# Layer 0's input transposed by VectorE from a second, rearranged load instead of by TensorE

## The chip, the cores and the metric

The kernel runs on one core of a Trainium2 chip. The metric is the device time of one execution in microseconds. The kernel before has a median of 2174.7 us over three runs (2173.53 to 2179.28); the profiled execution spans 2173.4 us.

## The reference, cut to what matters

Four graph layers follow one another over x of shape (128 graphs, 64 nodes, 256 features), each as `x = layernorm(x + layer(x))`. Only layer 0, an attention over the nodes of a graph, is touched:

```
Wh = einsum('bnf,fo->bno', x, W)                 # W is 256 x 256
e  = leaky_relu(Wh@a1 [:, :, None] + Wh@a2 [:, None, :], 0.2)
e  = where(adj == 0, -inf, e)
h  = einsum('bij,bjo->bio', softmax(e, -1), Wh)
x  = layernorm(x + h)
```

Layer 1 is a four-headed attention over 512 edges with a softmax over segments, layer 2 a normalised adjacency followed by two linear maps with batch statistics, layer 3 a graph convolution followed by short LSTMs. The projection `x @ W` needs x with features on the partitions, while x arrives in memory with one token per row.

## The kernel before, in words

**Tiling.** The 8192 tokens are cut in 16 blocks `q` of 512 tokens. A block is a tile `xin` of 128 partitions x 4 x 256: partition p of piece c holds token 128 c + p (two graphs per piece). `A` is one large tile, 128 x 16 x 1024, that holds the activations of all blocks in SBUF; block q's slice `A[:, q, :]` is first written when layer 0 of that block ends. Until then its upper end serves as room for set-up tiles (`su.tile`), taken from the top of A downwards.

**Layer 0** is cut in steps, each a function of a block:

- `load_x(q)` (lines 126 to 128) loads the block into one of two buffers `xin`;
- `l0_a` (208 to 210) calls `transposed` (191 to 199): for each half k of the features four TensorE transposes of 128 x 128 against an identity into one PSUM bank `m` (L197), and one ScalarE copy of the bank into `tT` (L198). Per block that is 8 transposes, 8 weight loads and 2 copies;
- `l0_b` (212 to 223) multiplies `tT` with the weights (L218) and copies out (L220, L223); `l0_c` makes scores and exponentials; `l0_d` transposes the exponentials; `l0_e` (252 to 266) multiplies by Wh (L258), adds the result to `xin` (L261, VectorE), normalises (L92 to L97) into `A[:, q, :]`, and calls `load_x(q + 2)`, since the buffer of `xin` is now free.

**Buffers.** `tT` has a single buffer, which `l0_a` shares with `l1_t`, the same helper in layer 1. So `l0_a`'s `tT` can be written only when the last reader of the previous one, `l1_qv` of the block before (L283 and L286), has finished. The PSUM pool `m` has three banks, used in turn by all of these steps.

**The loop** (lines 647 to 664) runs layers 0, 1 and the first part of 2 interleaved. Each turn q handles eight halves b of layer 1's edge scores (`l1_graph`, L320 with the ScalarE relu L322), and between them the steps in `between`. At b = 0 come `l0_e(q + 1)` and `l0_a(q + 2)`, at b = 2 `l0_b(q + 2)`. In every second turn the list holds layer 1's softmax too (`l1_softmax`, `l1_sums`, `l1_weights`: the VectorE scans L337 to L346 and the reciprocal L360).

**Order.** `step` ties every step's instructions on TensorE behind the step before it, by `tc.issue_after(queue[-1])`, so TensorE's order is the order of the list. On the other engines and on the queue that issues DMAs (SyncE) the framework's planner decides: it takes instructions in the written order as they become ready in its own forecast of time, so a later one whose inputs are there can go ahead of an earlier one that waits. Each engine then runs its list strictly in order.

Of the kernel before, what the change touches and what calls it, by code (L numbers as in the profile page):

```python
# [8 lines left out]
F32 = mybir.dt.float32  # L9
# [8 lines left out]
P = 128  # L18
# [3 lines left out]
KD = D // P  # L22
# [6 lines left out]
QT = 512  # L29
# [12 lines left out]
def kernel(ctx: ExitStack, tc: tile.TileContext, i, out):  # L42
    nc = tc.nc
# [8 lines left out]
    A = main.tile([P, NQ, 2 * QT], F32, name="A")  # L52
# [59 lines left out]
    with ExitStack() as two:  # L112
# [5 lines left out]
        work = ph.enter_context(tc.tile_pool(name="work", bufs=2))  # L118
        ps = ph.enter_context(tc.tile_pool(name="ps", bufs=1, space=PSUM))

        def bank(shape, name="m", bufs=3):
            return (psm if name == "m" else ps).tile([P] + shape, F32, name=name, bufs=bufs)
# [3 lines left out]
        def load_x(q):  # L126
            xin[q] = xp.tile([P, PQ, D], F32, name="xin")
            nc.sync.dma_start(xin[q], x_view[q])

        class su:  # L130

# [15 lines left out]


        load_x(0)
        w0 = wa.tile([P, KD, D + 2], F32, name="w0")  # L150
        nc.scalar.dma_start(w0[:, :, :D], i["L0_gnn_W"].rearrange("(k p) c -> p k c", p=P))
# [7 lines left out]
        for s in range(2):  # L159
            nc.sync.dma_start(bd[s * N:(s + 1) * N, s * N:(s + 1) * N], i["adj"])  # L160
        load_x(1)

        wq = wa.tile([P, KD, D + HEADS], F32, name="wq")
# [23 lines left out]
        def own(q, shape, name):  # L187

            return work.tile(shape, F32, name=name, bufs=1) if q else su.tile(shape, F32, name)

        def transposed(src, q=1):

            t = own(q, [P, KD, QT], "tT")
            for k in range(KD):
                p_ = bank([PQ, P])
                for c in range(PQ):
                    nc.tensor.transpose(p_[:, c, :], src[:, c, k * P:(k + 1) * P], ident)  # L197
                nc.scalar.activation(t[:, k, :], p_.rearrange("p c t -> p (c t)"), AF.Copy)  # L198
            return t
# [6 lines left out]
        L0 = {}  # L206

        def l0_a(q):
            L0[q] = {"x": xin.pop(q)}
            L0[q]["xT"] = transposed(L0[q]["x"], q)  # L210

        def l0_b(q):
            xT = L0[q]["xT"]
# [38 lines left out]
        def l0_e(q):  # L252
            x, wh, eT, ri = (L0[q][n] for n in ("x", "wh", "eT", "ri"))
            for c2 in range(2):
                p_ = bank([2, D])
                for c in range(2):
                    g = 2 * c2 + c
                    nc.tensor.matmul(p_[:, c, :], eT[:, g, :], wh[:, g, :D], start=True, stop=True)  # L258
                for c in range(2):
                    g = 2 * c2 + c  # L260
                    nc.vector.scalar_tensor_tensor(x[:, g, :], p_[:, c, :], ri[:, g:g + 1], x[:, g, :],  # L261
                                                   op0=OP.mult, op1=OP.add)
            layernorm(token_major(q), x, PQ, nc.gpsimd)
            L0.pop(q)
            if q + 2 < NQ:
                load_x(q + 2)
# [243 lines left out]
        def setup_signs():  # L510
# [4 lines left out]
            for h in range(HEADS):  # L515
                r, c0 = slice((h % 2) * 64, (h % 2 + 1) * 64), CG - HEADS + h
                nc.vector.tensor_copy(apad[r, h // 2, c0:c0 + 1], acol[r, h // 2:h // 2 + 1])

        l0_a(0)
        setup_l0()  # L520
        nc.vector.tensor_scalar(mask, bd, 0.0, NEG, op0=OP.is_equal, op1=OP.mult)
        l0_b(0)
        setup_order()
        l0_c(0)
        l0_a(1)
        setup_ends()
        l0_b(1)
# [119 lines left out]
        for q in range(NQ):  # L647
            S = q // BPS - 1 if q % BPS == 0 else -1
            between = [
                [(l0_e, q + 1), (l0_a, q + 2)],  # L650
                [(sums, q if q else -1), (l1_softmax, S)],
                [(l1_sums, S), (l0_b, q + 2)],
                [(v_b, q - LAG - 1)],
                [(l1_weights, S), (l1_t, q + 1), (l0_c, q + 2)],
                [(sums, q), (l1_qv, q + 1, 0)],
                [(v_c, q - LAG - 1), (v_a, q - LAG)],
                [(l0_d, q + 2), (l1_qv, q + 1, 1)],
            ]
            for b in range(GQ):
                step(l1_graph, q, b)  # L660
                for do, n, *more in between[b]:
                    step(do, n, *more)
                if setup:
                    setup.pop(0)()
# [58 lines left out]
        q = 0  # L723
# [90 lines left out]
    work = ctx.enter_context(tc.tile_pool(name="work3", bufs=2, reuse_waits="tile"))  # L814
# [290 lines left out]
```

## Time and profile before

| what | value |
|---|---|
| median of three runs | 2174.7 us |
| TensorE busy | 2083.1 us (96%) |
| ScalarE busy | 946.2 us (44%) |
| VectorE busy | 863.1 us (40%) |
| GpSimd busy | 414.7 us (19%) |
| DMA | 169275 packets, 105.54 MB |
| L197 transposes from `xin` | 128, median 273 ns each |
| L198 copies to `tT` | 62, mean 597 ns (both layers) |

Busy time is the union of an engine's instructions, so overlapping matmuls count once. Busy shares are averages over the whole span; layer 0 lies in the first quarter of it, so its stages must be read by themselves. In listings of one engine in order of time the columns are start, duration of the merged group, engine, line, operation, output and inputs, shape and count; a bracket gives idle time ahead of the group and what ended it.

### The profile page before, as it was taken

How to read it: one execution, taken by the hardware profiler on the slowest of the kernel's cores; microseconds unless marked ns; L12 is line 12 of the kernel's file. 1: busy time of each engine (PE TensorE's matmuls, PEld its weight loads, DVE VectorE, ACT ScalarE, POOL GpSimd, SP SyncE). 2: the span in 40 equal slices, each digit the busy share in tenths (PEclk: the TensorE clock that was granted, in tenths of full speed). 3: DMA queues.
4: the chain of work that ended last, by engine and by line, in shares of the span. 5: the costliest groups of instructions: out<-in, count | busy, mean ns of one | idle time of the engine just before them, and what ended most of it. 6: DMA issues, size and time to landing. Idle time of an engine off the chain costs nothing.

```text
span 2173.4 us, 29437 instructions
## 1 busy us (share of the span) xinstructions
PE 2083.1 (96%) x11463; PEld 1340.8 (62%) x11463; DVE 863.1 (40%) x2054; ACT 946.2 (44%) x1825; POOL 414.7 (19%) x569
## 2 busy tenths in 40 slices
PE   6999999998999979999999999999999999999997
PEld 4667677775454444576576577477468468468466
DVE  7355555454543444134233323323323423423223
ACT  3766666765338153234233334333333333333332
POOL 1123332433210012011111111111211211202012
PEclk9999999999999979999999999999999999999999
DMA  4023213232222022012112101201201201201001
GB/s 124 20 42 52 50 44 50 52 52 42 42 86 59 0 87 79 0 44 67 46 31 66 60 29 54 73 14 55 88 10 58 89 4 60 73 1 59 20 5 54
DMA packets 169275, 105.54 MB, mean 49 GB/s; under 512 B 86832, under 2 KB 152368, under 8 KB 168880
## 3 DMA queue, kind: packets, MB, share of 16 engines
q1 hardware_dynamic: 167280, 101.70, 17.7%
q8 instruction: 90, 1.47, 0.3%
q0 software_dynamic: 1024, 1.05, 0.2%
q10 hardware_dynamic: 832, 0.92, 0.1%
q14 instruction: 49, 0.40, 0.1%
HBM read 59.59 MB, written 44.04 MB: 48 GB/s over the span
## 4 chain that ended last, share of the span: by engine, by line
PE 80%; ACT 6%; DVE 6%; DMA 3%; issue 2%; POOL 1%; SPq 1%; DVEq 0%; POOLq 0%; ACTq 0%
PE l L970 31%; PE l L976 19%; PE pz L707 5%; PE pz L772 4%; PE e L311 3%; PE g L909 2%; PE g L921 2%; PE m L283 2%; PE m L218 2%; PE m L286 2%; PE g L866 1%; DMA way<-st 1%; PE z L320 1%; PE m L401 1%; PE m L197 1%
## 5 line engine op out<-in xcount | busy, mean ns | idle before, releaser
L970 PE MATMUL l<-H,wih 128*128 128x256 f32 (+2 forms) x2496 | 789.2, 471 | 9.4 <-ACT gate_g L990 3.9
L970 PEld LDWEIGHTS l<-H,wih 128*128 128x128 f32 x2496 | 469.9, 190 | 302.3 <-issue 189.2
L976 PE MATMUL l<-hid,whh 128*128 128x256 f32 (+2 forms) x1536 | 436.2, 437 | 2.1 <-DVE hid L999 2.1
L976 PEld LDWEIGHTS l<-hid,whh 128*128 128x128 f32 x1536 | 291.8, 190 | 130.9 <-issue 61.2
L982 ACT ACTIVATE gate_i<-l,bias 128x256 f32<-128x256 f32 (+2 forms) x176 | 100.1, 569 | 517.8 <-PE l L976 445.9
L985 DVE TENSOR_TENSOR gate_i<-gate_i,gate_g 128x256 f32<-128x256 f32 (+2 forms) x96 | 48.5, 506 | 432.7 <-ACT gate_g L982 432.6
L986 POOL TENSOR_TENSOR cell<-gate_f,cell 128x256 f32<-128x256 f32 (+2 forms) x96 | 84.4, 880 | 670.6 <-ACT gate_f L982 663.4
L83 POOL TENSOR_TENSOR ln_rs<-ln_rs,mhalf 128x2 f32<-128x2 f32 (+2 forms) x97 | 79.1, 815 | 689.5 <-DVE ln_rs L95 689.1
L322 ACT ACTIVATE u<-z 128x1024 f32<-128x1024 f32 x128 | 130.4, 1026 | 57.4 <-PE z L320 56.6
L982 ACT ACTIVATE gate_g<-l,bias 128x256 f32<-128x256 f32 (+2 forms) x176 | 100.3, 570 | 98.3 <-PE l L970 50.1
L990 ACT ACTIVATE gate_g<-cell 128x256 f32<-128x256 f32 (+2 forms) x176 | 90.0, 511 | 88.7 <-DVE cell L989 45.7
L982 ACT ACTIVATE gate_o<-l,bias 128x256 f32<-128x256 f32 (+2 forms) x176 | 99.4, 565 | 61.9 <-PE l L976 54.0
L707 PE MATMUL pz<-A,w 128*128 128x512 f32 x256 | 113.1, 595 | 0.0
L989 DVE TENSOR_TENSOR cell<-gate_i,gate_g 128x512 f32<-128x512 f32 (+2 forms) x80 | 50.0, 624 | 138.1 <-ACT gate_g L982 137.9
L294 DVE TENSOR_TENSOR qs<-m,qs 64x256 fp32r<-64x256 f32 x128 | 54.0, 422 | 124.4 <-ACT qs L293 122.7
L320 PE MATMUL z<-gath_r,qs 128*128 128x512 f32 x256 | 99.4, 476 | 0.6 <-ACT u L322 0.4
L707 PEld LDWEIGHTS pz<-A,w 128*128 128x128 f32 x256 | 47.9, 190 | 55.3 <-issue 53.6
L283 PE MATMUL m<-wq,tT 128*128 128x260 f32 x256 | 72.4, 406 | 8.1 <-ACT yT L391 5.4
L982 ACT ACTIVATE gate_f<-l,bias 128x256 f32<-128x256 f32 (+2 forms) x96 | 51.1, 532 | 59.8 <-PE l L976 59.8
L999 DVE TENSOR_TENSOR hid<-gate_o,gate_g 128x256 f32<-128x256 f32 (+2 forms) x96 | 48.6, 507 | 67.8 <-ACT gate_g L990 39.8
L999 DVE TENSOR_TENSOR H<-gate_o,gate_g 128x512 f32<-128x512 f32 (+1 forms) x64 | 40.9, 639 | 80.7 <-PE l L970 68.5
L286 PE MATMUL m<-wv,tT 128*128 128x256 f32 x256 | 67.3, 386 | 0.6 <-ACT v L296 0.5
(241 smaller groups left out, 2515.2 us busy)
## 6 DMA issues: line engine op xcount, KB each, us to landing
way<-st SPq DMA_DIRECT2D x59, 256.0 KB
st<-way SPq DMA_DIRECT2D x236, 64.0 KB
xin<-in_x SPq DMA_DIRECT2D x16, 512.0 KB
ld<-table SPq DMA_DIRECT2D x16, 512.0 KB
x_dram<-y SPq DMA_DIRECT2D x16, 512.0 KB
x2r<-x_dram SPq DMA_DIRECT2D x32, 256.0 KB
x_dram<-A SPq DMA_DIRECT2D x64, 128.0 KB
x3r<-x_dram SPq DMA_DIRECT2D x64, 128.0 KB
```

The costliest lines, as they stand in the source:

```text
L283: nc.tensor.matmul(pq, xT[:, k, c * P:(c + 1) * P], wq[:, k, :], start=k == 0, stop=k == KD - 1)
L286: nc.tensor.matmul(pv[:, c % 2, :], xT[:, k, c * P:(c + 1) * P], wv[:, k, :], start=k == 0, stop=k == KD - 1)
L320: nc.tensor.matmul(z[:, k, :], L1[q]["qs"][c][:, s, k * P:(k + 1) * P], gath_r, start=True, stop=True)
L322: nc.scalar.activation(u, z, AF.Relu)
L707: nc.tensor.matmul(p_, w1[:, k, m * P:(m + 1) * P], A[:, q, k * QT:(k + 1) * QT], start=k == 0, stop=k == KD - 1)
L772: nc.tensor.matmul(p_, w2[:, k, m * P:(m + 1) * P], hidden(q, k), start=k == 0, stop=k == M1 - 1)
L970: nc.tensor.matmul(gates[n], wih[p][:, k, mw * P:(mw + 1) * P], Hw[:, k, :, s, :], start=k == 0, stop=not s and k == KD - 1)
L976: nc.tensor.matmul(gates[n], whh[p][:, k, m * P:(m + 1) * P], hid[:, k], start=False, stop=k == KD - 1)
L982: nc.scalar.activation(act[n], gates[n], AF.Tanh if n == "g" else AF.Sigmoid, bias=bias[:, p - 1, m:m + 1])
L986: nc.gpsimd.tensor_tensor(cell[:, j], act["f"], cell[:, j], OP.mult)
L990: nc.scalar.activation(act["g"], cell[:, j], AF.Tanh)
L999: nc.vector.tensor_mul(Hw[:, jj, :, s, :] if over else new[:, jj], o, t)
```

## The change

`load_x(q)`, for every block but the first, loads the input a second time, into the still unused slice `A[:, q, :]`. Eight DMAs, one for each quarter n of the partitions and half k of the features, put into partition 32 n + t the pieces of 32 features (128 bytes) that start at feature 128 k + 32 n, of the tokens 32 j + t for j from 0 to 15. So each square of 32 partitions x 32 columns of A holds 32 tokens by 32 features, and already stands in the quarter of the partitions where its features belong. One VectorE transpose in squares of 32 then gives `tT` as before. TensorE's transposes and ScalarE's copies of `l0_a` go, for 15 of 16 blocks. The first load into `xin` remains, for the residual addition in `l0_e`. Its purpose is to take work off TensorE and ScalarE.

```diff
         def load_x(q):
             xin[q] = xp.tile([P, PQ, D], F32, name="xin")
             nc.sync.dma_start(xin[q], x_view[q])
+            if q:
+
+                rows = i["x"][q * QT:(q + 1) * QT, :].rearrange("(j t) (k i f) -> i k t j f", t=32, k=KD, f=32)
+                for n in range(4):
+                    for k in range(KD):
+                        to = A[n * 32:(n + 1) * 32, q, k * QT:(k + 1) * QT]
+                        nc.sync.dma_start(to.rearrange("t (j f) -> t j f", f=32), rows[n, k])
...
         def l0_a(q):
             L0[q] = {"x": xin.pop(q)}
-            L0[q]["xT"] = transposed(L0[q]["x"], q)
+            if q:
+
+                L0[q]["xT"] = work.tile([P, KD, QT], F32, name="tT", bufs=1)
+                nc.vector.transpose(L0[q]["xT"].rearrange("p k t -> p (k t)"), A[:, q, :])
+            else:
+                L0[q]["xT"] = transposed(L0[q]["x"], q)
```

## The prediction

> **What bounds the kernel now.** I first read the page's busy shares and its chain of work that ended last, then the first 600 us in stretches of 30 us, because layer 0 lives only there.
>
> ```profile
> PE 2083.1 (96%) x11463; PEld 1340.8 (62%) x11463; DVE 863.1 (40%) x2054; ACT 946.2 (44%) x1825; POOL 414.7 (19%) x569
> ...
> PE 80%; ACT 6%; DVE 6%; DMA 3%; issue 2%; POOL 1%; SPq 1%; DVEq 0%; POOLq 0%; ACTq 0%
> ```
>
> ```profile
> core 0: us, PE busy (x) PEld busy (x) DVE busy (x) ACT busy (x) POOL busy (x), PEclk, DMA share, GB/s
> 190.00:220.00 30.00, 29.22 (x275) 21.76 (x274) 13.05 (x41) 21.38 (x49) 12.32 (x16) 1.00 0.48 75
> 220.00:250.00 30.00, 27.66 (x258) 21.02 (x256) 18.31 (x40) 20.20 (x47) 6.95 (x8) 1.00 0.11 36
> ```
>
> TensorE (PE) is the bound in the loop too: 29.2 and 27.7 of 30 us. The second stretch is a turn with layer 1's softmax, where VectorE (DVE) is fuller. So TensorE time taken out comes off the end, if VectorE delivers in time. One turn without the softmax shows the room, first on TensorE, then on VectorE:
>
> ```profile
> 265.49 1.03 PE L286 MATMUL m<-wv,tT 128*128 128x256 f32 x4
> 266.17 0.81 PE L320 MATMUL z<-gath_r,qs 128*128 128x512 f32 x2
> 266.82 1.89 PE L258 MATMUL m<-wh,eT 128*128 128x256 f32 x8
> 268.89 1.09 PE L197 MATMUL m<-ident,xin 128*128 128x128 f32 x8 [0.18 <-ACT spad L295]
> 269.74 0.72 PE L320 MATMUL z<-gath_r,qs 128*128 128x512 f32 x2
> 270.39 1.92 PE L311 MATMUL e<-u,apad 128*32 128x512 f32 x16
> 272.24 0.73 PE L320 MATMUL z<-gath_r,qs 128*128 128x512 f32 x2
> 272.81 3.65 PE L218 MATMUL m<-w,tT 128*128 128x258 f32 x16
> ```
>
> ```profile
> 265.77 0.88 DVE L294 TENSOR_TENSOR qs<-m,qs 64x256 fp32r<-64x256 f32 x2 [0.62 <-ACT qs L293]
> 267.63 0.43 DVE L294 TENSOR_TENSOR qs<-m,qs 64x256 fp32r<-64x256 f32 x1 [0.98 <-ACT qs L293]
> 268.09 1.66 DVE L261 SCALAR_TENSOR_TENSOR xin<-m,ri,xin 128x256 f32<-128x256 f32 x4
> ...
> 271.52 0.16 DVE L95 TENSOR_SCALAR ln_rs<-ln_mv 128x4 f32<-128x4 f32 x1
> ```
>
> The last reader of `tT` (L286) ends at 266.52; L218, which needs the new `tT`, starts at 272.81. VectorE is idle from 266.65 to 267.63, then busy until 271.68.
>
> For the added work I read the same operation elsewhere, and the issues of the DMA queue:
>
> ```profile
> L848 DVE STREAM_TRANSPOSE st<-hd x31: 700/705/712, 948.3 to 2138.7; 128x512 f32<-128x512 f32 x31
> ```
>
> ```profile
> 8.94 0.47 SPq L77 DMA_DIRECT2D w<-in_W1T  x1
> ...
> 9.96 0.51 SPq L64 DMA_DIRECT2D b<-in_L_gnn_b  x1
> ...
> 38.14 0.37 SPq L128 DMA_DIRECT2D xin<-in_x  x1
> ```
>
> Vectors of layer 2 (L64), written after the whole loop, are loaded at 9.96 us, ahead of block 2's `xin`, which waits for its buffer. So the planner lets a load go as soon as its destination is free.
>
> **What the skill says.** (1) VectorE: DVE Perf Modes, The three transpose paths: VectorE's transpose works in blocks of 32 x 32 alone and writes SBUF. That is why the DMA must deal the features to the quarters. The trace has its time: 705 ns for 512 columns. (2) TensorE: Matmul & The Clock Gate, Part 4: PE-mode transpose: some 275 ns in a kernel, the result lands in PSUM and wants a copy, and transposes don't count as activity for the clock. The trace agrees on the first (273 ns median latency; eight overlap in 1.09 us) and leans to the last: in the softmax turn, after a stretch of almost only transposes from 246.05, L311 takes 3.09 us at 251.56 where 1.85 is usual. (3) DMA: Bandwidth & Descriptors, Specifications: full rate needs 512 bytes or more per descriptor. The trace agrees: the pairs of `ld` loads (L372: 8192 pieces of 128 bytes) run from about 141.0 to 148.3 at 122 to 188 GB/s, while `xin` reaches 244 to 364.
>
> **The change part by part.**
>
> *Removed from TensorE, in the loop (14 blocks, 2 to 15).* Eight transposes. L258 starts at 266.82 and ends at 268.71; in this sequence the next group starts 0.15 before the modelled end of the last, so L320 would start at 268.56 instead of 269.74: 1.18 us per turn, of which 0.18 is the wait for a PSUM bank (ACT L295) that the transposes were first to meet. *Removed from ScalarE*: two copies, 2 x 0.597 = 1.2 us per turn. ScalarE is at 20 to 21 of 30 us and its L322 is mostly waiting for TensorE, so I count this at nothing.
>
> *Added to VectorE.* One transpose of 1024 columns. The slope from L294 (256 columns, 422 ns) to a same-kind operation of 512 (L332, 0.69 us) is 1.05 ns per column, so 705 + 512 x 1.05 = 1.24 us; at most 2 x 0.705 = 1.41. It waits for the columns and for L286 of the previous `tT`, 266.52. In the planner's order L294, L261 and the normalisation are written earlier, but at 266.65 none of them is ready: the last L294 waits for ScalarE's L293, which in turn stands behind the copy of v (L296) that begins when L286 ends. I expect the transpose in this gap: about 266.65 to 267.95. Behind it the last L294 moves by some 0.4 us, and so do L261 and the normalisation; the next reader of that L294, an L320 six halves on, and ScalarE's L295, which runs at 268.67 anyway, don't feel it. L218 could start at 271.63: 3.7 us of slack. In a softmax turn the same gap lies at 231.15 to 232.13; L95 then ends near 236.6, and L332, which waits for L330 (now ending 1.18 earlier, at 236.7), starts in time. So 1.18 in both kinds of turn.
>
> *Added DMAs.* Per block 8 x 512 = 4096 pieces of 128 bytes, 0.5 MB: half of an `ld` pair, so 7.3 / 2 = 3.7 us of all DMA engines, and 8 issues. At the median of the `st` loads (L853, 428 ns) that is 3.4 us of SyncE. For 15 blocks: 61440 pieces, 7.9 MB, 55 us of DMA and 51 of SyncE. Slices of A below the set-up room are free from the start, so by the L64 evidence most columns will be loaded in the first 100 us or so, tens of microseconds before use, and before the first `ld` at 139.5. Even if issued right after their `xin` (209.76 for the block used at 233.4), they land by about 209.8 + 0.4 + 3.4 + 3.7 = 217. Hidden, then.
>
> *Set-up (block 1) and the first turns.* From 10 to 50 us VectorE is the bound (9.89, 7.01, 9.96 and 8.46 of 10 us), and TensorE's eight transposes at 18.17 are hidden there: nothing is won and 1.24 us of VectorE added. Block 1's columns follow `xin` at 6.86, so they are issued to about 10.7 and land near 15; `acol`, read by VectorE at 15.25, is pushed from 7.28 to about 11. Bounds: 0 (VectorE's gaps between 20 and 30 us take it) and 3 us (a wait as well). I take 1. In the two first turns set-up still fills VectorE, so I count 0.5 each instead of 1.18.
>
> *Sum.* 12 x 1.18 + 2 x 0.5 - 1 = 14.2; 2174.7 - 14.2 = 2160.5 us.
>
> **Rivals.**
>
> *A: the transpose falls behind the normalisation.* If the planner's forecast has no gap, it starts at 271.68 and ends at 272.92, and L218 starts 0.1 to 0.3 later than before (semaphore included). In softmax turns it lies between L95 (236.18) and L332, which starts at 237.5 instead of 237.9: 0.2 to 0.4 won. With 7 turns of each and 1 us of set-up: 2174.7 + 2.1 - 1.4 + 1 = 2176. For it: L261 is written first. Against: the 0.98 us gap.
>
> *B: softmax turns give nothing.* Their VectorE is busy from 237.90 to 253.5 almost without a break, and TensorE waits there in small pieces (0.57 for L403, 0.45 for L93); a longer wait can bring the slow clock. Six full turns: 7.1 + 1 - 1 = 7.1 won, 2167.6.
>
> *C: the columns come late, slower.* SyncE is in order and waits up to 23.6 us for L403, up to 19.8 for the table. If the columns of every second block stand behind the `ld` loads (263.80 to 267.15), they follow that pair's transfer (7.3 us from about 265.3, so to 272.6) by 3.7, to 276.3; with 1.24 for the transpose L218 starts at 277.6, 4.8 later than before. 7 x 4.8 - 7 x 1.18 + 1 = 26: 2201. Against: a free destination.
>
> **How the numbers follow.** Forecast 0.62, A 0.15, B 0.13, C and other losses in set-up 0.10. The best case is 14 x 1.27 with some luck in the clock, about 2154; the upper end takes in B and A, with 2177. Under 2168.2 (0.3%): 0.62 and most of B, 0.72. Within: A and the rest of B, 0.17. Slower: 0.11.
>
> **What would show it.** L197 from `xin` x8 instead of x128; a VectorE STREAM_TRANSPOSE x15 of about 1.24 us at the new line, ahead of L261, waiting for TensorE's L286 and not for a DMA; L320 directly behind L258; no TensorE wait before L218; the two kinds of turns, 29.8 and 35.5 us between L197 groups (203.62, 233.39, 268.89), shorter by 1.2 each; the new issues mostly before 110 us. Wrong would be: a wait of L218 for VectorE (A), TensorE idle growing near L403 and L229 (B), a VectorE wait for a DMA into A (C), or a loop that starts more than 3 us later.

## The result, and the profile after

The changed kernel takes 2157.5 us, median of four runs (2154.84 to 2158.79), against 2176.23 us of the kernel before on the same chip. The ratio is 0.9912, with a 95% interval of 0.9894 to 0.9930: faster by 0.9%. 2160.5 was forecast.

The page of the changed kernel, busy shares and the chain of work that ended last (its line numbers are those of before + 7 from `load_x` on, + 12 behind `l0_a`):

```profile
PE 2066.8 (96%) x11343; PEld 1329.6 (62%) x11343; DVE 881.6 (41%) x2069; ACT 931.1 (43%) x1795; POOL 418.7 (19%) x569
...
PE 81%; DVE 7%; ACT 5%; DMA 3%; issue 2%; POOL 1%; SPq 0%; ACTq 0%; DVEq 0%; POOLq 0%
```

TensorE has 120 matmuls and 16.3 us less, ScalarE 30 instructions and 15.1 us less, VectorE 15 instructions and 18.5 us more (15 x 1.24 = 18.6). TensorE is still the bound at 96%, with a shorter span (2156.5 against 2173.4 us in the profiled executions). One turn without the softmax, on TensorE in order of time:

```profile
317.18 0.82 PE L332 MATMUL z<-gath_r,qs 128*128 128x512 f32 x2
317.83 1.89 PE L270 MATMUL m<-wh,eT 128*128 128x256 f32 x8
319.37 0.82 PE L332 MATMUL z<-gath_r,qs 128*128 128x512 f32 x2
320.12 1.92 PE L323 MATMUL e<-u,apad 128*32 128x512 f32 x16
321.97 0.73 PE L332 MATMUL z<-gath_r,qs 128*128 128x512 f32 x2
322.54 3.65 PE L230 MATMUL m<-w,tT 128*128 128x258 f32 x16
```

L332 stands directly behind L270, 1.54 us after its start; before, its counterpart L320 came 2.92 us after L258's start. L230 has no bracket: no wait took the place of the transposes. From L270's start to L230's it is 4.71 us, before 5.99. VectorE in the same turn:

```profile
316.77 0.88 DVE L306 TENSOR_TENSOR qs<-m,qs 64x256 fp32r<-64x256 f32 x2 [0.62 <-ACT qs L305]
317.68 1.25 DVE L220 STREAM_TRANSPOSE tT<-A 128x1024 f32<-128x1024 f32 x1
318.96 0.43 DVE L306 TENSOR_TENSOR qs<-m,qs 64x256 fp32r<-64x256 f32 x1
319.42 1.66 DVE L273 SCALAR_TENSOR_TENSOR xin<-m,ri,xin 128x256 f32<-128x256 f32 x4
...
322.85 0.16 DVE L95 TENSOR_SCALAR ln_rs<-ln_mv 128x4 f32<-128x4 f32 x1
```

The transpose fills the gap ahead of the last L306, and ends 3.6 us before L230 wants `tT`. L306 and L273 come 0.32 us later after L270's start than before (1.13 against 0.81, 1.59 against 1.27), and no wait of TensorE follows from that. The groups of the transposes and, in the queue's own view, of the second loads, with counts and durations in ns (least, median, most), first and last start:

```profile
L220 DVE STREAM_TRANSPOSE tT<-A x15: 1240/1245/1245, 22.8 to 440.2; 128x1024 f32<-128x1024 f32 x15
```

```profile
L135 SPq DMA_DIRECT2D A<-in_x x120: 312/487/1842, 7.2 to 279.3; - x120
```

To compare kernels I measure turns from one start of `l0_e`'s matmuls (L258, now L270) to the next. The first column is the end of set-up, at block 0's `l0_e`; the second is block 1's, with which the loop begins. Of the turns the table has the regular ones, five of each kind, and it shows why a turn is a better ruler than a median: turns without the softmax agree within 0.03 us between executions.

| kernel | set-up to the first L258 | the loop's first L258 | turns without softmax | turns with softmax | layer 2's first matmul | ratio to before, 95% |
|---|---|---|---|---|---|---|
| before | 28.60 | 53.96 | 29.77 | 33.9 x3, 35.5 x2 | 541.82 | |
| after | 31.11 | 56.59 | 28.49 | 32.75 x5 | 523.62 | 0.9894 to 0.9930 |
| after, again | 33.08 | 56.95 | 28.49 | 32.75 x5 | 520.38 | 0.9912 to 0.9942 |
| e1 | 29.61 | 53.48 | 28.50 | 32.75 x5 | 517.00 | 0.9878 to 0.9911 |
| e2 | 28.64 | 54.05 | 29.78 | 33.9 x3, 35.5 x2 | 542.07 | 1.0010 to 1.0023 |
| e3 | 30.82 | 56.38 | 28.50 | 32.75 x4, 34.2 | 521.27 | 0.9884 to 0.9916 |
| e4 | 32.76 | 56.64 | 29.77 | 33.9 x4, 35.5 | 540.41 | 0.9989 to 1.0002 |
| e5 | 33.77 | 59.33 | 30.0 to 30.15 | 33.07 to 33.54 | 540.93 | 1.0023 to 1.0040 |
| e6 | 37.01 | 62.58 | 28.50 | 40.8 to 43.0 | 591.05 | 1.0201 to 1.0250 |
| e7 | 33.72 | 59.02 | 29.91 to 30.07 | 33.3 | 549.22 | 1.0028 to 1.0059 |
| f1 | 31.31 | 56.43 | 28.50 | 33.3 x3, 33.5, 35.0 | 533.08 | 0.9978 to 0.9992 |
| f2 | 32.50 | 58.07 | 28.50 | 32.77 x4, 32.9 | 526.03 | 0.9911 to 0.9949 |
| f3 | 28.98 | 54.51 | 28.49 | 32.75 x5 | 522.06 | 0.9889 to 0.9918 |
| f4 (e1 again) | 29.15 | 54.16 | 28.50 | 32.75 x5 | 520.69 | 0.9879 to 0.9916 |

Turns of 35.5 us, and the odd 34.2 and 35.0, hold a stretch at a slow TensorE clock (before, 317.2 to 319 us: 0.55 of full speed granted; usual: 1.00).

### The profile page after: what moved, and what is told of

The parts are those of the page before. It is cut to its first block, busy times and chain, and to the rows that moved or that the text cites. A ratio compares the mean times of both kernels' runs of the same rounds, so it can differ in the third digit from the quotient of the medians.

```text
span 2156.5 us, 29415 instructions
## 1 busy us (share of the span) xinstructions
PE 2066.8 (96%) x11343; PEld 1329.6 (62%) x11343; DVE 881.6 (41%) x2069; ACT 931.1 (43%) x1795; POOL 418.7 (19%) x569
## 4 chain that ended last, share of the span: by engine, by line
PE 81%; DVE 7%; ACT 5%; DMA 3%; issue 2%; POOL 1%; SPq 0%; ACTq 0%; DVEq 0%; POOLq 0%
PE l L982 32%; PE l L988 19%; PE pz L719 5%; PE pz L784 4%; PE e L323 3%; PE g L921 2%; PE g L933 2%; PE m L295 2%; PE z L332 2%; PE m L298 2%; PE m L230 2%; PE g L878 1%; PE m L413 1%; DMA way<-st 1%; ACT A L891 1%
## 5 line engine op out<-in xcount | busy, mean ns | idle before, releaser
L334 ACT ACTIVATE u<-z 128x1024 f32<-128x1024 f32 x128 | 130.3, 1025 | 64.3 <-PE z L332 63.3
L332 PE MATMUL z<-gath_r,qs 128*128 128x512 f32 x256 | 100.9, 482 | 0.6 <-ACT u L334 0.4
L306 DVE TENSOR_TENSOR qs<-m,qs 64x256 fp32r<-64x256 f32 x128 | 54.1, 422 | 109.0 <-ACT qs L305 106.9
L721 DVE BATCH_NORM_STATS2 st<-pz 128x6 f32<-128x512 f32 x64 | 44.4, 697 | 59.5 <-PE pz L719 59.4
```

The costliest lines, as they stand in the source:

```text
L332: nc.tensor.matmul(z[:, k, :], L1[q]["qs"][c][:, s, k * P:(k + 1) * P], gath_r, start=True, stop=True)
L334: nc.scalar.activation(u, z, AF.Relu)
```

## The experiments

Theory: the gain is the time of eight transposes on a full TensorE, and it is whole because the VectorE transpose lands in a gap and the loads are hidden. Rivals: the gain is ScalarE's relief; the loads, or block 1, take back a part of it; the place on VectorE is of no weight.

**The changed kernel again**, beside the next three on one chip.

> The changed kernel once more, as the measure for the three beside it. Every theory: about 2157 us, 17 to 19 below the kernel before on the same chip.

Measured: 2156.38 us (before there: 2173.99). The result repeats.

**Dead TensorE transposes (e4).** The part of the gain that is TensorE's.

```diff
                 nc.vector.transpose(L0[q]["xT"].rearrange("p k t -> p (k t)"), A[:, q, :])
+                for k in range(KD):
+                    p_ = bank([PQ, P])
+                    for c in range(PQ):
+                        nc.tensor.transpose(p_[:, c, :], L0[q]["x"][:, c, k * P:(k + 1) * P], ident)
```

> The changed kernel, and in addition TensorE makes the eight transposes of each block as before, into PSUM banks that nothing reads; ScalarE's copies stay away. Theory 1 (the gain is TensorE's time): 14 x 1.1 to 1.2 us come back, so 2172 to 2176. Rival (the gain is ScalarE's relief, or a shorter chain to tT): stays at 2157 to 2162.

Measured: 2173.03 us against 2173.85, ratio 0.9995. TensorE in order of time:

```profile
360.05 1.89 PE L274 MATMUL m<-wh,eT 128*128 128x256 f32 x8
362.12 1.10 PE L224 MATMUL m<-ident,xin 128*128 128x128 f32 x8 [0.18 <-ACT spad L311]
362.98 0.70 PE L336 MATMUL z<-gath_r,qs 128*128 128x512 f32 x2
```

The group of 1.1 us and even its wait of 0.18 for a PSUM bank are back, and the regular turns are those of before to 0.03 us, slow stretches apart. The whole gain in them is TensorE's time. That the medians agree too is in part luck: e4's loop starts 2.7 us later than before's (56.64 against 53.96), and its first three turns are 3.0 us shorter together (85.2 against 88.2), because slow stretches that before has there are missing.

**Dead ScalarE copies (f2).** The complement.

```diff
                 nc.vector.transpose(L0[q]["xT"].rearrange("p k t -> p (k t)"), A[:, q, :])
+                for k in range(KD):
+                    nc.scalar.activation(A[:, q, k * QT:(k + 1) * QT], L0[q]["x"][:, 2 * k:2 * k + 2, :].rearrange("p c d -> p (c d)"), AF.Copy)
```

> The changed kernel, and in addition two ScalarE copies of 128 x 512 per block where the old ones stood, from xin into the already read slice of A, which nothing reads. Theory 1 (ScalarE's copies were hidden): 2156 to 2159, turns of 28.5 and 32.75 us. Rival (part of the gain is ScalarE's): 2160 to 2170, turns longer by up to 1.2.

Measured: 2161.35 us (2157.26 to 2162.0). By its time alone that is the rival's range, not the theory's. But the rival put the loss in the turns, and these are 28.50 and 32.77, those of the changed kernel: the copies cost these turns nothing. Its ratio to before (0.9911 to 0.9949) overlaps that of the changed kernel's repeat, and what its median has over 2157.5 lies outside the regular turns, spread too thin to be placed (the loop's first group at 58.07 against 56.59 and 56.95; from the last group of the loop to layer 2 55.3 us against 54.8 and 52.5; behind it 1634 against 1633).

**Loads without their use (e2).** `load_x` as in the change, `l0_a` as before.

```diff
         def l0_a(q):
             L0[q] = {"x": xin.pop(q)}
-            if q:
-                L0[q]["xT"] = work.tile([P, KD, QT], F32, name="tT", bufs=1)
-                nc.vector.transpose(L0[q]["xT"].rearrange("p k t -> p (k t)"), A[:, q, :])
-            else:
-                L0[q]["xT"] = transposed(L0[q]["x"], q)
+            L0[q]["xT"] = transposed(L0[q]["x"], q)
```

> The columns are loaded into A, but nothing reads them: xT comes from TensorE as before. Theory 1 (the loads are hidden): within 2 us of the kernel before, about 2176. Rival (61440 small pieces slow the other transfers or hold SyncE, and part of the gain pays for that): 4 to 10 us above the kernel before.

Measured: 2177.45 us against 2173.99, ratio 1.0016 (1.0010 to 1.0023), so 2 to 5 us more, between the two theories. But in the profile, which caught the slowest of the 20 executions (2181.27), layer 2 begins at 542.07, before at 541.82: the stage with the loads lost 0.25 us. The rest took 1637.4 instead of 1631.6, though no load of the change is left there and TensorE, ScalarE and GpSimd run the whole kernel in the order of before. So the loads are hidden where they run. Of the 5.8 us behind, 3.3 arise at one place near 1530 us. There VectorE's addition of `st`, a tile that is written to memory and read back, waits for its DMA, in before and in e2:

```profile
1529.69 0.69 DVE L884 TENSOR_TENSOR x2r<-st,x2r 128x512 f32<-128x512 f32 x1 [2.37 <-DMA st<-way]
```

```profile
1532.28 0.69 DVE L891 TENSOR_TENSOR x2r<-st,x2r 128x512 f32<-128x512 f32 x1 [4.00 <-DMA st<-way]
```

The `H` that TensorE needs stands behind it in VectorE's order, so TensorE waits 2.39 us instead of 0.76, and matmuls of 1.06 us instead of 0.70 follow. Another 1.0 arises in the same way near 1025 us. Over all profiles here these two waits of TensorE run from 0.5 to 2.4 us. With one profile of each kernel it stays open whether the loads have a part in that, and what the 2 to 5 us of the 20 executions are.

**No second load (e3).** VectorE transposes `xin` itself.

```diff
-            if q:
-                rows = i["x"][q * QT:(q + 1) * QT, :].rearrange("(j t) (k i f) -> i k t j f", t=32, k=KD, f=32)
...
-                nc.vector.transpose(L0[q]["xT"].rearrange("p k t -> p (k t)"), A[:, q, :])
+                nc.vector.transpose(L0[q]["xT"].rearrange("p k t -> p (k t)"), L0[q]["x"].rearrange("p c d -> p (c d)"))
```

> No second load; VectorE transposes xin itself in squares of 32, so the features are not dealt to their quarters and layer 0's projection reads another arrangement (this part of the computation is changed). TensorE, ScalarE and VectorE do the work of the changed kernel. Theory 1 (loads hidden): within 2 us of the changed kernel, about 2157, a little less if the loads hold up set-up. Rival (the loads cost): 4 to 10 us below the changed kernel.

Measured: 2151.46 us, 4.9 below the changed kernel beside it, which favoured the rival. But its turns are those of the changed kernel, one slow stretch apart, and its loop starts at 56.38, within 0.6 us of the changed kernel's two executions; what it has won lies behind layer 1 (1629.5 against 1633.7), where no load of the change runs and all engines have the same order, at the two waits named under e2. That called for a second pair, e1 with and without loads:

**No second load, block 1 on TensorE (f3), beside e1 again (f4).** The edits are those of e3 and e1 together.

> As e1 (block 1 on TensorE), but VectorE transposes xin itself and there is no second load, so the features aren't dealt to their quarters (this part of the computation is changed). Beside f4 it prices the loads alone. Theory 1 (hidden): within 1 us of f4 in the loop, and in all within the 3 us by which executions differ. Rival (the loads cost 3 to 5 us, as the medians of e2 and e3 suggest): 2145 to 2147.

> e1 once more, the fastest kernel so far: 2149 to 2152. If its 6.6 us below the changed kernel were partly chance of the clock, it lands at 2152 to 2155.

Measured: 2154.61 us without the loads, 2153.09 with them. Without block 1 the loads cost nothing that can be measured: 1.5 us, to the other side. The rival of 3 to 5 us falls. f4 itself came 3.3 above e1's first median, on another chip, in the range that was named for a part of chance; its ratio to before (0.9897) is near e1's (0.9894).

**Block 1 back on TensorE (e1).**

```diff
-            if q:
+            if q > 1:
```

in `load_x` and in `l0_a`.

> Block 1 goes back to TensorE transposes and gets no second load; blocks 2 to 15 are as in the changed kernel. Theory 1 (block 1 wins nothing, since TensorE isn't the bound during set-up, and its VectorE transpose starts the loop later by the 2.6 us seen between the first L258 and L270 groups of the loop, 53.96 and 56.59): 2 to 3 us below the changed kernel, about 2154.5. Rival (the late start is made up for later, because turns 0 to 2 were 2 to 5 us shorter after it): within 1 us of the changed kernel.

Measured: 2149.75 us, 6.6 below the changed kernel beside it, where 2 to 3 were expected; ratios to before 0.9894 and, repeated, 0.9897, against 0.9912 and 0.9927 of the changed kernel. In the profiles 3.5 us of the 6.6 are there from the loop's first group on (53.48 against 56.95) and stay to layer 2 (517.00 against 520.38); the other 3 come behind layer 1, where both run the same order, again at the waits named under e2. So the late start isn't made up for, and the rival falls. The table shows the size of the step: the loop's first group comes at 53.5 to 54.5 us in the five executions with block 1 on TensorE (before, e1, e2, f3, f4) and at 56.4 to 58.1 in six with block 1 on VectorE (twice the changed kernel, e3, e4, f1, f2). That is 1.9 to 4.6 us, and it is the VectorE transpose and not the loads: e2, which has only the loads, is at 54.05, and e3, which has only the transpose, at 56.38. e1's is the lowest median here. What block 1 does, on TensorE, in the changed kernel, in the one before and in e1:

```profile
24.05 5.44 PE L230 MATMUL m<-w,tT 128*128 128x258 f32 x16 [2.33 <-DVE ri L254]
```

```profile
23.25 3.73 PE L218 MATMUL m<-w,tT 128*128 128x258 f32 x16
```

```profile
24.26 3.73 PE L230 MATMUL m<-w,tT 128*128 128x258 f32 x16
```

In the changed kernel L230 of block 1 waits until VectorE, busy with set-up, has made `tT` (22.75 to 23.99; the bracket names `ri`, the next that VectorE ends). Behind the idle time it runs at a slow clock, 0.59 of full speed granted and then 0.80, where before and e1 have 1.00 for the same group: 5.44 us for work of 3.73. It takes 5.2 us or more in all nine profiles with block 1 on VectorE and 3.73 in all five with it on TensorE.

**The transpose behind the normalisation (e5).** My rival A, built.

```diff
-                nc.vector.transpose(L0[q]["xT"].rearrange("p k t -> p (k t)"), A[:, q, :])
+                dve = [t for t in nc.cur_bb.bb.instructions if t.engine == mybir.EngineType.DVE]
+                with tc.issue_after(dve[-1]):
+                    nc.vector.transpose(L0[q]["xT"].rearrange("p k t -> p (k t)"), A[:, q, :])
```

> The VectorE transpose is tied behind the last instruction of the normalisation of the block before (L95), in place of the gap ahead of L273. My prediction's rival A, worked out there: L230 waits for VectorE in turns without the softmax, and L344 is held up in the others; about 2174 to 2177. Rival theory (the place is of no weight, TensorE has other work): 2157 to 2160.

Measured: 2181.95 us (20 runs, 2172.5 to 2184.48) against 2173.85: slower than before, and 5 above the range expected. VectorE, then TensorE, in a turn without the softmax:

```profile
336.94 1.24 DVE L222 STREAM_TRANSPOSE tT<-A 128x1024 f32<-128x1024 f32 x1
```

```profile
338.32 3.73 PE L232 MATMUL m<-w,tT 128*128 128x258 f32 x16 [1.27 <-DVE tT L222]
```

The wait takes the place of the transposes: 1.27 us for 1.28. The turns without the softmax are 30.0 to 30.15, 0.2 to 0.4 longer than before; rival A said 0.1 to 0.3. The softmax turns, 33.1 to 33.5, keep only part of their gain. The profiled execution, 2172.5 us, was the fastest and had a mean granted clock of 0.987; the others had 0.980 to 0.986 and took 2 to 12 us more, so the profile doesn't show what the median has above the range.

**Doubled loads (e6).**

```diff
                         nc.sync.dma_start(to.rearrange("t (j f) -> t j f", f=32), rows[n, k])
+                        nc.sync.dma_start(to.rearrange("t (j f) -> t j f", f=32), rows[n, k])
```

> Every column load is issued twice: 16 DMAs and 8192 pieces of 128 bytes per block. In this kernel's order on VectorE the planner puts the transpose of every second block behind the softmax scans (L358's counterpart), since it forecasts the columns late. Theory 1 (a transfer's time is hidden, but a late place on VectorE is not): L230's counterpart in softmax turns waits some 6 us more, 6 or 7 x 5 to 6 us: 2185 to 2200. Rival (the doubled loads are hidden and the order has no weight): 2157 to 2162.

Measured: 2223.59 us, 50 more than before, beyond what I expected. VectorE, then TensorE, in a softmax turn:

```profile
338.02 1.22 DVE L221 STREAM_TRANSPOSE tT<-A 128x1024 f32<-128x1024 f32 x1
```

```profile
339.38 6.35 PE L231 MATMUL m<-w,tT 128*128 128x258 f32 x16 [8.35 <-DVE tT L221]
```

The transpose doesn't wait for its columns here: it starts when the scans end, and no bracket with a DMA stands at it. The planner has put it behind the scans in VectorE's fixed order. TensorE then waits 8.35 us, not the 6 I had assumed, and its clock drops (0.50 granted, 6.35 us for 3.65). In the other turns, where the transpose keeps its gap, they are 28.50: twice the loads are hidden too.

**Two transposes into tT (e7), and a second one into A (f1).** Both put a second transpose in the same place on VectorE, inside the normalisation; in f1 it writes the slice of A that has been read, so no matmul depends on it.

```diff
                 nc.vector.transpose(L0[q]["xT"].rearrange("p k t -> p (k t)"), A[:, q, :])
+                nc.vector.transpose(L0[q]["xT"].rearrange("p k t -> p (k t)"), A[:, q, :])
```

> The VectorE transpose is made twice, one behind the other in the written order; in the planner's order the second lands inside the normalisation. It asks how much VectorE time is left. Theory 1: turns without the softmax have room (no loss), softmax turns have none, since L344 already starts within 0.3 us of L95: 6 or 7 x 0.9 to 1.25 us, so 2163 to 2167. Rival (VectorE has room everywhere): 2157 to 2159.

```diff
                 nc.vector.transpose(L0[q]["xT"].rearrange("p k t -> p (k t)"), A[:, q, :])
+                nc.vector.transpose(A[:, q, :], A[:, q, :])
```

> The changed kernel, and a second VectorE transpose per block that writes into the already read slice of A instead of tT, so that no matmul waits for it; VectorE's order has it in the same place as e7, inside the normalisation. Theory 1 (e7 lost its time because L231 waited for the second writing of tT, not for want of VectorE time): turns without the softmax stay at 28.5 us, softmax turns grow by up to 1.25, in all 2157 to 2165. Rival (VectorE has no time left in any turn): 2180 to 2187, as e7.

Measured: e7 2184.68 us, f1 2171.83 us (profiled: 2167.3). e7's expectation missed by 18 us: I had asked for VectorE's room and had built another late `tT`, since L231 must wait for the second writing (the bracket names the small operation right behind it); the turns without the softmax lost 1.4 us:

```profile
282.20 3.73 PE L231 MATMUL m<-w,tT 128*128 128x258 f32 x16 [1.17 <-DVE ln_mv L93]
```

f1 asks the question properly, and there they keep 28.50: in these VectorE has room for a second transpose. Softmax turns grow from 32.75 to 33.32 and more, so there it hasn't. The two early turns, still full of set-up, lose most (from the third to the fifth L258-like group f1 takes 63.0 us, after 54.9), which I had not expected; that puts f1 above its range.

## Why the prediction was right, step by step

**TensorE's transposes.** 1.18 us per turn forecast; 1.28 in turns without the softmax, 1.15 in softmax turns at full clock. e4's regular turns give all of it back. The 0.18 us wait for the bank did go with them.

**ScalarE at nothing.** Right: f2's turns are those of the changed kernel.

**VectorE's 1.24 us in the gap.** Right in size (1.245), in place, and in what hides it. In softmax turns 0.1 us of slack was forecast ahead of L332, now L344: it is 0.13 (290.25 to 290.38). e5 shows that the place decides: rival A would have been the result otherwise, with 2182 worse than the 2176 I gave it.

**The loads.** Hidden, as e2's loop, f3 against f4 and the 28.50 us turns of e6 show. But the planner didn't pull most of them into the first 100 us, as I concluded from the layer 2 vectors: 49 of the 120 are issued by 103 us, the last at 279.3, and block 15's are read only at 440.2. They keep a few blocks ahead. The second argument, that a load right behind its `xin` is early enough, would have carried the step alone. Rival C exists as an order of instructions (e6), not as a late transfer.

**Set-up.** The term was mis-sized: 1 us forecast, 2.6 and 3.0 measured at the loop's first group (56.59 and 56.95 against 53.96). That is just under the 3 us that I had named as a sign of being wrong. The 1 was VectorE's time; TensorE's wait stood in the upper bound alone, and the slow clock behind it nowhere. e1 takes the step back.

**The sum.** By the two profiles the 14 turns with a transpose gave 23.0 us, where 12 x 1.18 + 2 x 0.5 = 15.2 was forecast. The excess is the clock, for the most part. Two softmax turns of before held a slow stretch, and the changed kernel had none: 3.2. Of the two early turns that I counted at 0.5 each, the first came out 0.5 longer and the second (80.33 to 109.95, now 83.42 to 108.41) 4.63 shorter. TensorE there, before and after:

```profile
89.70 0.46 PE L616 MATMUL m<-A 128*128 128x128 f32 x2 [2.75 <-DVE A L614]
...
90.10 5.33 PE L218 MATMUL m<-w,tT 128*128 128x258 f32 x16
```

```profile
89.81 0.49 PE L628 MATMUL m<-A 128*128 128x128 f32 x2 [1.19 <-DVE A L626]
...
90.25 3.65 PE L230 MATMUL m<-w,tT 128*128 128x258 f32 x16
```

Of the 4.63, 1.4 are transposes, 1.68 are L218's slow clock, and 1.56 are TensorE's wait for set-up (L616, now L628). The wait goes with the transposes: it is 2.75 to 2.94 in before, e2 and e4, which have them on TensorE, and 1.17 to 1.19 in both executions of the changed kernel and in e1, e3, f2, f3 and f4 (e5 to e7 and f1, which put the transpose elsewhere or add another, have 0.8 to 5.6). The slow clock doesn't: e4, with the transposes, has that group at 3.65.

Against the 23.0 stand set-up with 2.6, the end of layer 1 with 2.2 (L323 at 3.64 instead of 1.92 us, a slow stretch again) and 1.3 behind layer 1. 23.0 - 2.6 - 2.2 - 1.3 = 16.9, the difference of the profiled spans (2173.4 and 2156.5); the medians differ by 18.7. The mechanism's part is, by my estimate, eight turns of 1.28 and six of 1.15 less set-up, 17.1 - 2.6 = 14.5. That this meets the forecast 14.2 is luck in part: too little for the two early turns and too little for set-up cancel. Of the 2.4 to 4.2 us beyond it, 1.56 are the wait above; the rest depends on where the clock's slow stretches and the waits of later layers happen to fall, and the edits did not settle whether the change causes that.

## What to carry to other kernels

Moving work from a full engine to one with room paid here what the full engine spent, because the moved instruction landed in a gap of the other's fixed order; look for that gap in order of time, next to the last reader of the buffer that it writes, before trusting busy shares. A few microseconds later in the same list the same instruction turns the gain into a wait. Leave out of such a change the iterations where the receiving engine is the bound, here block 1 in set-up.

## What was not expected of the hardware

The time of an execution goes with its mean granted clock. Over the 40 runs of the kernel before beside e4 a clock lower by 0.001 goes with 1.5 us more, and the executions spread from 2168.64 to 2179.75 us. Idle time of TensorE is often followed by slow matmuls: block 1's L230 took 5.44 and 6.47 us in two executions, e6's L231 6.35, where 3.65 is usual. Which softmax turns fall to the slow clock wasn't settled. With layer 0's transposes on TensorE it is five of fifteen (before, e2, e4); without them it is two of forty (one each in e3 and f1, none in the changed kernel's two executions, e1, f2, f3 and f4; e5 to e7 are left out, since their softmax turns differ otherwise). That fits what the prediction read in the Trainium skill, that transposes don't count as activity for the clock (TensorE: Matmul & The Clock Gate, Part 4: PE-mode transpose). But no edit tested it by itself, and e3 and f1 have the slow stretch without these transposes.

Loads in pieces of 128 bytes were no threat here, since they were early: twice 61440 of them left the turns that didn't depend on the planner's forecast at 28.50 us.
